# Queries of two batches from seven block products for eight, the second batch's queries and the summed weights kept in DRAM: a fused gated cross-attention and LoRA-MoE kernel

## The chip, the cores and the metric

The kernel runs on one core of one Trainium2 chip. The metric is the device time of one execution in microseconds. The kernel before takes 2636.26 us, the median of three runs (2635.27, 2636.26 and 2637.21).

The engines have short names throughout. PE is TensorE, the matrix engine, and PEld its weight loads. DVE is VectorE, ACT is ScalarE and POOL is GpSimd. SP is SyncE, which issues most of the DMA transfers (SPq is its queue). "Granted clock" is the share of full speed at which TensorE was allowed to run.

## The reference, cut to what matters

Everything is fp32. `x` is (4, 256, 512): four batches of 256 query rows. `ctx` is (4, 1601, 512): 1601 context rows for each batch. There are 32 query heads and 8 key/value heads of 128 columns, so G = 4 query heads share a key/value head.

```python
q = (layernorm(x) @ Wq + bq).reshape(B, L, 8, 4, 128)      # Wq: 512 x 4096
k, v = split(ctx @ Wkv + bkv, 2)                            # Wkv: 512 x 2048
scores = einsum('blkgd,bmkd->bkglm', q, k) / sqrt(128)
o = einsum('bkglm,bmkd->blkgd', softmax(scores), v)
x = x + tanh(g_xattn) * (o.reshape(B, L, 4096) @ Wo + bo)
h = layernorm(x)
w = top-2-of-8 weights of softmax(h @ router_W.T), renormalised
x = x + tanh(g_ffn) * (h @ base_W.T + 2 * sum_e w_e * (h @ A_e) @ B_e)   # rank 16
```

Only the computation of `q` and the handling of the projection weights change here.

## The kernel before, in words

**Tiling.** One group is one batch b, one key/value head h and one tile l of 128 query rows: 4 x 8 x 2 = 64 groups, worked one after another. A group's 4 query heads x 128 rows are the 512 columns of its score products. The 1601 context rows are 12 tiles of 128 and a rest of 65, so a group has 13 score products (`score_unit`) and 13 products of probabilities with values (`av_unit`). The maximum over the context rows is folded tile by tile on DVE and spread over the partitions (`fold`, `spread`). Then DVE subtracts it (`sub`, L925) and ACT takes the exponent (`exp`, L928). An fp32 product takes two passes, which are two MATMUL records in the trace.

**Order of the work.** `run_group` puts the score products of one group on PE, in turns with the AV products of the group before. After it, `window` puts filler on PE, until about RATE ns of it have been placed: keys, values and queries that later groups need, and the output projection of the group before. Filler is a list of `Task`s, each a list of steps with a cost and, for some, a due window. The orders of PE, DVE and ACT are written out by hand (`tc.manual_schedule`). At build time, a planner keeps a model clock for each engine (`clock`) and decides in which order instructions are emitted. Work for DVE and ACT is put off into named queues by `later` ("sub", "oT", "exp", "ln", "T", "sum", "low"). `pump` emits pieces as the model clock passes them; `force` emits what a piece needs, along with pieces of other queues that fit before it within FIT ns. On the chip, each engine works strictly through the order that came out of this.

**Keys and values.** Most of them are made with the Strassen-Winograd scheme: a product of 2x2 blocks takes seven block products and some additions instead of eight block products (`pair_steps`, L645). The blocks of the weight are two heads by two halves of the 512 input features (A11, A12, A21, A22). The other factor is split by the same halves of the features and by two halves of the context rows. Four sums of weight blocks (`weight_sums`, L306: S1, S2, S4 and S3, which overwrites A21) and the sums of context blocks (`ctx_sums`) are made on DVE, in queue "T". The results pass through PSUM banks named `px`, `py` and `pz`. ACT copies a finished one out, and DVE adds a bank to what was copied (`copy_to`, `add_to`). The key and value weights are loaded again and summed again for every batch (`load_pair`, L293).

**Queries.** `q_steps` (L532) makes the queries of one key/value head in one batch: 4 heads x 4 chunks of 128 features, as 16 plain products of 256 columns into the banks `pq`, and ACT copies each with its bias into `qT` (L547). `load_wq` (L282) loads the 1 MB of weights of a head. `x_steps` (L383) loads the x of a batch, layer-normalises it (`layernorm`: statistics on DVE, the root on ACT, then reciprocal and normalisation on DVE, all by `later`), transposes it on PE (`transpose_rows`, L248, bank `pt_x`) and copies it out on DVE as `xnT`.

**The start.** For batch 0, the kernel transposes context tiles as they land (`turn_ctx`), and makes the keys and values of the first head pair by plain products (`pk`, `pv`) as soon as a tile allows it. From the seventh tile on it adds the x steps, and then come the four query products of head 0 and the first scores. The loads of the start are all issued at once, mostly on SP, in the order context tiles, value weights, more context tiles, x, query weights.

## Time and profile before

| | before |
|---|---|
| median of three runs | 2636.26 us |
| profiled execution | 2636.84 us |
| its span | 2635.1 us |
| mean granted TensorE clock | 0.999 |
| PE busy | 2608.0 us, 99%, 9125 instructions |
| PEld busy | 1480.3 us, 56% |
| DVE busy | 2090.8 us, 79%, 2991 instructions |
| ACT busy | 1187.5 us, 45%, 1896 instructions |
| POOL busy | 96.4 us, 4%, 400 instructions |
| DMA | 104.71 MB, mean 40 GB/s |
| score products (L889) | 775.6 us |
| AV products (L979) | 766.1 us |
| query products (L540) | 231.5 us, 1024 records |
| output projection (L1052) | 231.5 us, 512 records |

Busy time is the time in which at least one instruction of the engine was running. Loads of PE weights run beside products and are counted apart. The span goes from the first to the last instruction of the profiled execution, which lasted 1.7 us longer than its span. A row of the group list gives source line, engine, operation, output and inputs with their shapes, the count, busy time, mean duration of one, and the idle time that lay ahead of it with what ended it. Records of products overlap each other, so a mean duration of a product is a latency and not the distance from one product to the next.

### The profile page before, as it was taken

The page shows a single profiled execution, that of the slowest core. Times are in us where ns is not written, and L with a number is a line of the kernel's source. Part 1 is how long each engine was busy: PE and PEld are TensorE (multiplying, and loading weights), DVE is VectorE, ACT ScalarE, POOL GpSimd, SP SyncE. Part 2 cuts the span into 40 slices and gives each one's busy share as a digit, 9 for nine tenths or more (in the row PEclk, how much of TensorE's full clock was granted, in tenths as well). Part 3 has the DMA queues.
Part 4 walks back from the last instruction along what each step waited for, and adds up shares of the span by engine and source line. Part 5 has one row for each costly group of instructions (what it writes and reads, how often), then busy time and mean ns, then how long its engine had stood idle before and what let it go on. Part 6 is the DMA issues. An engine that isn't in the chain of part 4 may idle for free.

```text
span 2635.1 us, 25287 instructions
## 1 busy us (share of the span) xinstructions
PE 2608.0 (99%) x9125; PEld 1480.3 (56%) x9125; DVE 2090.8 (79%) x2991; ACT 1187.5 (45%) x1896; POOL 96.4 (4%) x400
## 2 busy tenths in 40 slices
PE   8999999999999999999999999999999999999998
PEld 6555565655646555565555646555565555646544
DVE  2787877888878887878878878888878878878886
ACT  2544444454444444446444444445544444444441
POOL 0000000000000000000000000000000000000000
PEclk9999999999999999999999999999999999999999
DMA  4101101120111101112001111002111011101100
GB/s 148 35 9 40 40 33 40 41 75 24 40 32 41 37 12 40 40 33 90 24 24 41 40 32 41 26 23 69 61 33 41 8 40 41 39 33 40 49 1 32
DMA packets 78150, 104.71 MB, mean 40 GB/s; under 512 B 3228, under 2 KB 36028, under 8 KB 78024
## 3 DMA queue, kind: packets, MB, share of 16 engines
q1 hardware_dynamic: 76632, 102.01, 12.1%
q8 instruction: 72, 1.18, 0.2%
q0 software_dynamic: 336, 0.55, 0.1%
q10 hardware_dynamic: 1056, 0.52, 0.1%
q14 instruction: 54, 0.44, 0.1%
HBM read 100.98 MB, written 2.10 MB: 39 GB/s over the span
## 4 chain that ended last, share of the span: by engine, by line
PE 80%; DVE 12%; ACT 5%; issue 1%; POOL 1%; DMA 0%; ACTq 0%; POOLq 0%; DVEq 0%
PE av L979 21%; PE sc L889 21%; PE po L1052 8%; PE pq L540 7%; PE pxk L674 5%; PE pxv L685 4%; PE pk L584 3%; DVE p L925 3%; ACT p L896 3%; PE pyk L674 2%; PE pyv L685 2%; DVE sm L821 2%; DVE mx L821 2%; ACT p L928 1%; PE pzk L674 1%
## 5 line engine op out<-in xcount | busy, mean ns | idle before, releaser
L889 PE MATMUL sc<-qT,kT 128*128 128x512 f32 (+1 forms) x1664 | 775.6, 592 | 1.3 <-ACT qT L547 1.3
L896 ACT COPY p<-sc 65x512 f32<-65x512 f32 x820 | 464.5, 589 | 680.4 <-PE sc L889 399.9
L979 PE MATMUL av<-p,v 65*128 65x512 f32 x1640 | 766.1, 592 | 2.0 <-ACT p L928 2.0
L979 PEld LDWEIGHTS av<-p,v 65*128 65x128 f32 x1640 | 309.5, 190 | 382.6 <-issue 378.2
L889 PEld LDWEIGHTS sc<-qT,kT 128*128 128x128 f32 (+1 forms) x1664 | 307.1, 186 | 375.2 <-issue 339.8
L821 DVE TENSOR_TENSOR mx<-mx,p 128x1024 f32<-128x1024 f32 x252 | 308.8, 1225 | 228.2 <-ACT p L896 225.8
L928 ACT ACTIVATE p<-p 65x512 f32<-65x512 f32 x442 | 434.4, 995 | 112.5 <-DVE p L925 104.8
L925 DVE TENSOR_TENSOR p<-p,mb 65x512 f32<-65x512 f32 x442 | 481.3, 1137 | 0.2
L821 DVE TENSOR_TENSOR sm<-sm,p 128x1024 f32<-128x1024 f32 x252 | 307.1, 1218 | 1.2
L1052 PE MATMUL po<-wo,oT 128*128 128x512 f32 x512 | 231.5, 595 | 0.0
L540 PE MATMUL pq<-xnT,wq 128*128 128x256 f32 x1024 | 231.5, 379 | 0.0
L540 PEld LDWEIGHTS pq<-xnT,wq 128*128 128x128 f32 x1024 | 193.2, 190 | 38.8 <-issue 5.1
L1052 PEld LDWEIGHTS po<-wo,oT 128*128 128x128 f32 x512 | 95.3, 191 | 103.1 <-issue 98.9
L712 ACT ACTIVATE kT<-pxk,biasT 128x384 f32<-128x384 f32 (+1 forms) x120 | 60.7, 526 | 183.2 <-PE pxk L674 183.2
L715 ACT COPY v<-pxv 128x384 f32<-128x384 f32 x120 | 56.9, 474 | 172.6 <-PE pxv L685 172.6
L838 POOL COPY quad_sm<-quad_sm 32x16 f32<-32x16 f32 x186 | 48.2, 259 | 2288.6 <-DVE quad_sm L834 2247.0
L815 DVE TENSOR_TENSOR mx<-p,p 128x1024 f32<-128x1024 f32 x63 | 77.2, 1226 | 58.5 <-ACT p L896 58.5
L547 ACT ACTIVATE qT<-pq,biasT 128x256 f32<-128x256 f32 x128 | 60.5, 473 | 136.5 <-PE pq L540 135.6
L685 PEld LDWEIGHTS pxv<-wv,ctxT 128*128 128x128 f32 x720 | 88.7, 192 | 20.2 <-issue 17.2
L685 PE MATMUL pxv<-wv,T 128*128 128x128 f32 x720 | 91.4, 277 | 4.2 <-ACT v L715 4.2
L584 PE MATMUL pk<-ctxT,wk 128*128 128x417 f32 (+1 forms) x256 | 91.7, 513 | 2.8 <-ACT ctxT L250 1.5
L685 PEld LDWEIGHTS pxv<-wv,T 128*128 128x128 f32 x720 | 86.3, 192 | 7.3 <-ACT v L715 6.5
(211 smaller groups left out, 2251.1 us busy)
## 6 DMA issues: line engine op xcount, KB each, us to landing
wq<-in_L_xattn_Wq_dram SPq DMA_DIRECT2D x32, 1024.0 KB, 5.2
wo<-in_L_xattn_Wo_dram SPq DMA_DIRECT2D x32, 1024.0 KB, 5.1
ctx<-in_ctx_dram SPq DMA_DIRECT2D x36, 256.0 KB, 2.6
wk<-in_L_xattn_Wkv_dram SPq DMA_DIRECT2D x30, 256.0 KB, 2.9
wv<-in_L_xattn_Wkv_dram SPq DMA_DIRECT2D x30, 256.0 KB, 3.3
ctx<-in_ctx_dram SPq DMA_DIRECT2D x6, 512.0 KB, 11.7
xa<-in_x_dram SPq DMA_DIRECT2D x4, 512.0 KB, 11.3
out_dram<-xa SPq DMA_DIRECT2D x8, 256.0 KB, 2.0
```

The costliest lines, as they stand in the source:

```text
L540: nc.tensor.matmul(pq[:, :L], w_t["q", b, h][:, c, g * HDIM : (g + 1) * HDIM], xnT_t[b][:, c, :], start=(c == 0), stop=(c == NC - 1),)
L584: nc.tensor.matmul(pk[:, :n], w_t["k", b, h // 2][:, raw_slot(h % 2, c), c % 2, :], ctxT_t[b][:, c, lo : lo + n], start=(c == 0), stop=(c ...
L674: nc.tensor.matmul(bk[:, :n], a(SLOT[i], c), operand(i, c, s, n), start=first and c == 0, stop=c == 1, skip_group_check=True,)
L685: nc.tensor.matmul(bk[:, t * HDIM : (t + 1) * HDIM], operand(i, c, s + t * P, P), a(SLOT[i], c), start=first and t == 0 and c == 0, stop=c ...
L815: nc.vector.tensor_tensor(acc, p[first], p[first + 1], op)
L821: nc.vector.tensor_tensor(acc, acc, p[j], op)
L889: nc.tensor.matmul(sc[:r, :], kT_t[b, h][:, key_col(i) : key_col(i) + r], qT_t[b, h][:, :, l * P : (l + 1) * P], start=True, stop=True,)
L896: nc.scalar.copy(p[:r, k, :], sc[:r, :])
L925: nc.vector.tensor_tensor(p, p, m, ALU.subtract)
L928: nc.scalar.activation(p, p, AF.Exp, scale=scale)
L979: nc.tensor.matmul(av, v_t[b, h][:r, i, :], p_t[key][j][:r, k, :], start=(j == 0 and k == 0), stop=(j == NPAIR - 1 and k == len(pairs[j]) ...
L1052: nc.tensor.matmul(po, oT_t[key][:, g, :], w_t["o", b, h][:, g, :], start=(g == 0), stop=(g == G - 1),)
```

## The change: what it does

- `x_steps` handles two batches at once (JOINT = 2). Their normalised, transposed x lie side by side in one tile `xq`, together with three sums; a fourth overwrites a block. The sums are made on DVE in queue "ln". x of batches 2 and 3 is made from head 3 of batch 1 on.
- The queries are made by `pair_steps("q", ...)`: the blocks of the weight are two heads by two halves of the features, and the columns' halves are the two batches. Fourteen products of 256 columns give two heads of two batches. The first batch's results go to `qT`, the second's to a tile `qs` and from there to DRAM, from where `load_q` reads them when their batch is worked. So `q_steps` comes only in batches 0 and 2, in every window, as a `first` task.
- `keep` writes a weight with its sums to DRAM when it is first used. `load_pair` reads it back in later batches, and `weight_sums` is left out then. The query weights' sums are made in queue "ln".
- RATE is 9700 for 10700, and `force` lets pieces of queue "sub" fit within 1200 ns.
- At the start, query weights of two pairs are loaded and their sums are put in the queue ahead of the context tiles; the x steps come from the fourth tile on; each key and value step comes one tile later; two query pairs precede the first scores.
- Space: the bias row `bo` goes into `qs`; tiles of the last part (`ones`, `fT`, `lm`, `midT`, `lm6`, the last output weight) lie in the tiles of `xq` and `wq`. Six early transposes of the feed-forward part are copied by ACT instead of DVE.

The core of the diff:

```diff
-            for other in queues.values():
+            for name, other in queues.items():
+                fit = 1200 if name == "sub" else FIT
...
-    def load_pair(kind, b, hp, tile_=None, eng=nc.sync):
+    def load_pair(kind, b, hp, tile_=None, eng=nc.sync, tag=None):
...
+        if (kind, hp) in kept:
+            eng.dma_start(w.rearrange("p s c f -> p (s c f)"), kept[kind, hp])
+            done["w", kind, b, hp] = clock["now"] + LAG_PAIR
+            return
+        src, lo = (wq, 0) if kind == "q" else (wkv, KVD if kind == "v" else 0)
...
+    def keep(kind, b, hp):
+        if (kind, hp) in kept or b == B - 1:
+            return
+        kept[kind, hp] = d = dram.tile([P, 14 * HDIM], F32, tag=f"w{kind}_{hp}", name=f"kept_{kind}_{hp}")
+        nc.sync.dma_start(d, w_t[kind, b, hp].rearrange("p s c f -> p (s c f)"))
 
     def weight_sums(kind, b, hp):
+        if ("w", kind, b, hp) in done:
+            return
...
-                "T", "v", 420, clock["now"] + LAG_PAIR,
+                "ln" if kind == "q" else "T", "v", 420, clock["now"] + LAG_PAIR,
...
+    JOINT = 2
+    TQ = JOINT * L // 2
+    XQ = NC * 2 * TQ + 6 * TQ
...
+        def sums():
+            xt, T = xnT_t[b], Tx_t[b]
+            b11, b12, b21, b22 = (xt[:, c : c + 2, k : k + TQ] for c in (0, 2) for k in (0, TQ))
+            for out_, x_, y_ in (
+                (T[:, 0], b12, b11),
+                (T[:, 1], b22, T[:, 0]),
+                (T[:, 2], b21, T[:, 1]),
+                (b12, b22, b12),
+            ):
+                later(
+                    "ln", "v", 160 + 2.1 * TQ, clock["v"],
+                    lambda o=out_, x=x_, y=y_: nc.vector.tensor_tensor(o, x, y, ALU.subtract),
+                    ("T", "q", b) if out_ is b12 else None,
+                )
...
-    def q_steps(b, h):
...
+    def load_q(b, h):
+        new_q(b, h)
+        for g in range(0, G, 2):
+            nc.sync.dma_start(qT_t[b, h][:, g : g + 2, :], q_kept[b, h, g])
...
@@ pair_steps
+            if is_q:
+                g = h0 % G + f
+                if JOINT == 1:
+                    return [(qT_t[b, h0 // G][:, g, half * TQ : half * TQ + n], bk[:, :n])]
+                if half == 0:
+                    return [(qT_t[b, h0 // G][:, g, :], bk[:, :n])]
+                return [(second["q"][:, f, :], bk[:, :n])]
...
-                over()
+                if i == 1 and s == parts0:
+                    keep(kind, b, hp)
+                    if is_q:
+                        if hp % 2 == 0:
+                            new_q(b, hp // 2)
+                        if JOINT == 2:
+                            second["q"] = pool.tile([P, 2, L], F32, tag="qs", name=f"qs_{nm}", bufs=1)
...
+                        nc.sync.dma_start(d, second["q"])
+                over()
...
-            done["xT", nm] = transpose_rows(xn, P, xT, f"f_{nm}")
+            done["xT", nm] = transpose_rows(xn, P, xT, f"f_{nm}", i is not None)
...
-    RATE = 10700
+    RATE = 9700
...
+    def q_steps(b, h, i):
...
+            if (b, hp) == (0, 0):
+                next_weights("q", 0, 2)
+            elif hp + 1 < NHEAD // 2 and (b, hp) != (0, 1):
+                next_weights("q", b, hp + 1)
+
+        return pair_steps("q", b, hp, then)[0]
...
-    load_wq(*heads[0])
+    load_pair("q", 0, 0)
+    load_pair("q", 0, 1, tag="wo")
...
+    ks, vs = plain_k_steps(0, 0), plain_v_steps(0, 0)
+    for i in range(NL):
+        weight_sums("q", 0, i)
...
-        if n >= 6 and xs:
+        if n >= 3 and xs:
             xs.pop(0)[2]()
-        if (n_k + 1) * SUB <= (i + 1) * P and i < FULL:
+
+        if (n_k + 1) * SUB <= i * P and i < FULL:
...
-    for f in qs:
-        spend(f[0])
-        f[2]()
-    load_wq(*heads[1])
+    for i in range(NL):
+        tasks.append(Task(q_steps(0, 0, i)))
+    flush(lambda t: True)
...
-            if h == NKV - 2 and l == 1 and b + 1 < B:
-                tasks.append(Task(x_steps(b + 1), now + 1))
+            if (h, l) == (NKV - 5, 1) and b + 1 < B and (b + 1) % JOINT == 0:
+                load_pair("q", b + 1, 0)
+                tasks.append(Task(x_steps(b + 1), now + 7))
...
-                tasks.append(Task(q_steps(*nxt), hi * NL + NL - 1))
+            if nxt is not None and nxt[0] % JOINT == 0:
+                tasks.append(Task(q_steps(*nxt, l), now, first=True))
+            elif nxt is not None and l == 0:
+                load_q(*nxt)
```

## The prediction

> **What bounds the kernel now.** I read the page's busy shares first, then what PE waits for, then single windows, and last the start.
>
> ```profile
> PE 2608.0 (99%) x9125; PEld 1480.3 (56%) x9125; DVE 2090.8 (79%) x2991; ACT 1187.5 (45%) x1896; POOL 96.4 (4%) x400
> ...
> PE pxv L685 <- ACT v L715: 4.2, 12, 0.6
> PE pt_f L248 <- DVE ffn_x L1155: 2.7, 1, 2.7
> ```
>
> PE is busy 99% of the span, and the longest wait in the list of its waits is 4.2 us in total. So the kernel is bound by how much PE has to do. DVE, at 79%, is next.
>
> The second view is the time line of PE, which gives the true rate of the Q projection; the means of the groups (379 ns) are latencies of overlapping instructions.
>
> ```profile
> 599.66 1.89 PE L540 MATMUL pq<-xnT,wq 128*128 128x256 f32 x8
> 601.39 0.60 PE L248 MATMUL pt_x<-ident,xn 128*128 128x128 f32 x4
> ```
>
> Eight records are four fp32 products of 256 columns (two passes each). From start to next start they take 1.73 us: 0.432 us a product. In the same way 512 columns cost 0.858, 417 cost 0.70, 384 cost 0.66 and 128 cost 0.112.
>
> The third view is the windows: a group's 13 score products with the 13 AV products of the group before (22.3 us), then filler (keys, values, Q, output), until the next group's first score. Four windows in a row:
>
> ```profile
> 798.40:842.00 43.60, 43.29 (x202) 28.27 (x201) 36.43 (x52) 20.61 (x33) 2.81 (x12) 1.00 0.07 25
> 842.00:877.90 35.90, 35.90 (x139) 21.02 (x137) 28.56 (x39) 15.36 (x24) 0.00 (x0) 1.00 0.14 44
> 877.90:919.50 41.60, 41.60 (x114) 21.14 (x113) 33.28 (x48) 20.98 (x33) 1.78 (x6) 1.00 0.08 26
> 919.50:955.10 35.60, 35.60 (x97) 18.10 (x96) 27.64 (x38) 13.82 (x22) 1.14 (x6) 1.00 0.14 44
> ```
>
> The columns after the length are PE, PEld, DVE and ACT busy. PE is busy from end to end. My per-product times, added up over the program order, give 43.1, 35.9, 41.7 and 35.8 for these windows, so sums of products are times here. DVE has 7 to 8 us idle in each.
>
> **What is removed: 64 products.** Before, 32 heads x 4 batches x 4 chunks = 512 products of 256 columns. After, two heads and two batches go together: 7 block products of two chunks, 14 for 16. That is 32 pairs x 14 = 448, and the built program has 448 of them, all 128x256. 64 x 0.432 = 27.65 us less PE work. If nothing else moved: 2636.84 (the profiled execution) - 27.65 = 2609.2.
>
> **What it adds off PE.** DVE: 96 additions of 128x256 (nearest rows: 128x384 takes 546 to 558 ns, 128x32 174 to 181; by line 0.42) = 40 us; weight sums go from 108 to 92 (405 ns each) = -6.5; eight sums of x halves at about 0.69 = 5.5. In all +39 us, in the even batches only, where the windows also gain PE work (14 products, 6.05 us, for 8, 3.46 us). ACT: 128 copies of Q before and after, 473 ns each. DMA: 23 stores and 36 loads of kept weights (0.92 MB), 32 stores and 32 loads of Q (0.26 MB), less 33.5 MB of Wq and 10.5 of Wkv, plus 8.4 of Wq in pair form: about 140 MB for 104.7, so the 12.1% share of the queue becomes about 17%. I cost this at nothing. What hides it is that a weight is loaded when the pair before it ends, about 40 us before its first use, and a 1 MB load lands in 5.2 us. On SP each store stands ahead of later loads and waits for sums on DVE. The tightest case is the key load of the second pair in batch 0: it stands behind the store of the fourth Q weight, whose sums lie behind seven subtractions. It is issued some 18.7 us after the last score, lands 4 us later, and DVE takes it up about 24.5 us after it: 2 us spare. Without that cover the folds behind these sums, and then the scores, would be late by the difference.
>
> Inside a Q pair the second block accumulates on the first one's bank, so PE needs ACT's copy of it first. ACT starts 0.20 us after the last product, runs 0.47, and PE resumes within 0.1: 0.75 us, against one product pair of 0.864 between. It fits if ACT is free, which it is at the start of a window (exponents come after the 4 us in which DVE spreads the maximum). Cost between 0 and 3 x 0.1 x 32 = 10 us; I take 1.
>
> **What it moves: the start.** This is where I see the gain go. Before:
>
> ```profile
> 8.58 1.11 PE L248 MATMUL pt_ctx<-ident,ctx 128*128 128x128 f32 x4
> 10.68 5.90 PE L584 MATMUL pk<-ctxT,wk 128*128 128x417 f32 x8 [0.99 <-DVE ctxT L253]
> 30.43 0.63 PE L248 MATMUL pt_x<-ident,xn 128*128 128x128 f32 x4 [1.53 <-DVE xn L272]
> 63.64 6.65 PE L889 MATMUL sc<-qT,kT 128*65 128x512 f32 x15 [0.56 <-ACT qT L547]
> ...
> 26.88 0.20 ACT L275 ACTIVATE sd_x<-sd_x 128x1 f32<-128x1 f32 x1
> 28.94 0.69 DVE L253 COPY ctxT<-pt_ctx 128x512 f32<-128x512 f32 x1 [6.28 <-PE pt_ctx L248]
> 29.55 0.15 DVE L271 RECIPROCAL rs_x<-sd_x 128x1 f32<-128x1 f32 x1
> ```
>
> The last three rows show DVE taking instructions strictly in order: the reciprocal had its input at 27.1 and ran at 29.55, after a copy that waited for PE. In the changed program DVE's order, after its second context copy (done at 10.4), is: eight sums of the first two Q weights, then the first layer norm, then everything else. And PE's order has the first x transpose, which needs that norm, ahead of the first key product. The Q weights are the last loads issued, behind all context tiles and two x tiles.
>
> ```profile
> 8.54 2.02 SPq L388 DMA_DIRECT2D xa<-in_x_dram  x1
> ...
> xa<-in_x_dram SPq DMA_DIRECT2D x4, 512.0 KB, 11.3
> ...
> 12.00:28.00 16.00, 15.21 (x59) 10.65 (x58) 1.63 (x4) 4.61 (x11) 0.00 (x0) 1.00 1.05 398
> ...
> q10 hardware_dynamic: 1056, 0.52, 2.5%
> ```
>
> The first x lands at 8.54 + 11.3 = 19.8. Then 0.52 MB more of x at 398 GB/s, 1.3 us; then 1.05 MB of Wq in rows of 512 bytes (before: 2 KB). q10 carried the key weights in such rows: 2.5% of 16 engines over 70 us for 0.52 MB is 300 GB/s, so 3.5 us. The Trainium skill (DMA: Bandwidth & Descriptors, Specifications) gives full line rate from 512 bytes up: 0.9 us less. I take the trace: both weights are there at 24.6. Four sums of 405 ns: 26.3. Statistics 1.05, root on ACT 0.4, reciprocal, norm and hand-over 0.9: PE goes on at 28.7, where before it went on at 10.7.
>
> From 28.7 to the first score PE has 50.9 us of work: four x transposes 1.8, keys 10.9, values 22.5, context transposes 3.6, Q 12.1. The first key group runs at half rate (5.7 us for 2.8), with the x transpose before it 3.4 us; before too. Each of the three later x transposes waits for a norm whose root stands on ACT behind the value copies: about 2.1 us each, by the rows above (1.53 for the same chain). Another 1.1 for the last key group, 1.5 inside the last Q pair, whose blocks have nothing between them. First score at 28.7 + 50.9 + 3.4 + 9.0 = 92.0, against 63.64: 28.4 later, of which 6.1 is work that is in the sum already (5.2 of Q, 0.9 of x). Stall added: 22 us. Bounds 14 (weights 3 us earlier, half of the later waits) and 29.
>
> A rule speaks against these gaps: by TensorE: Matmul & The Clock Gate (The HAM clock gate, "What's actually happening") an idle window of about 3.4 us drops PE to half clock, and it takes as long to recover. By the rule the three gaps of 2.1 us cost nothing more. The trace is less lenient:
>
> ```profile
> 2524.82 1.57 PE L248 MATMUL pt_f<-ident,ffn_x 128*128 128x128 f32 x8 [2.74 <-DVE ffn_x L1155]
> 2526.18 4.86 PE L1052 MATMUL po<-wo,oT 128*128 128x512 f32 x8
> ...
> 2526.00:2528.00 2.00, 2.00 (x5) 0.96 (x4) 1.78 (x4) 0.00 (x0) 0.00 (x0) 0.50 0.03 8
> ```
>
> A gap of 2.74 us was followed by a granted clock of 0.50 and 4.86 us for what takes 3.60; one of 2.10 us at 2486 was not. I take 0, and keep 3 x 1.7 = 5 for the range.
>
> **The middle and the end.** In batches 1 and 3 Q comes from DRAM, so four windows have 156.7 - 4 x 3.46 = 142.9 us of PE work, 35.7 each; DVE has 125.9 - 8 x 0.405 = 122.7, 30.7 each. Waits on POOL and on copies leave it a little room: 1 us in all. At the end 6.9 us of Q filler are gone from the windows where PE already stands 9.6 us for DVE (time line of PE, 2459 to 2544), but six copies of 0.69 move from DVE to ACT: between -4 and +6, I take +1.
>
> **Sum.** 2636.84 - 27.65 + 22 + 1 + 1 + 1 = 2634.2; the median before is 0.6 below the profiled execution: 2633.6, say 2634. About 5.3 us (0.2%) is what a measurement of this kernel can tell from no change: 2631.0 to 2641.5.
>
> **The rivals.**
> (A, 40%) The sum above: the start eats four fifths of the gain, 2628 to 2641.
> (B, 33%) The start costs half of what I say, because the weights land earlier than first in, first out (two key pieces issued into an empty queue landed after 3.7 and 5.7 us). For: the queue's engines work side by side. Against: x took 10.9 to 11.7 us in this very place. 11 us back: 2623.
> (C, 18%) DVE becomes the bound in batches 1 and 3. For: 30.7 us busy; maximum folds now wait (225.8 + 58.5) / 64 = 4.4 us per window for score copies, POOL 1.0; if these waits stay, 36.1, and with 0.3 for the projections 36.4 is over 35.7. It decides from there: 0.7 x 28 windows = 20 us, 2654. Against: the waits shrink when DVE is late, and up to seven score banks can wait before PE does.
> (D, 9%) Copies inside the Q pairs come late, behind exponents: 0.3 us per pair and more, 2644.
> That the change leaves the products as they were is excluded by the program's own count.
>
> **Numbers.** Faster: B nearly whole and a sixth of A, 0.38. Same: most of A and a little of D, 0.35. Slower: C and most of D, with A's upper edge, 0.27. Range for 8 in 10: 2620 (B with its lower bounds) to 2653 (most of C).
>
> **What would show it.** In the profile after: PE idle about 18 us before its first x transpose, released by DVE xn, with DVE waiting for a DMA of wq; first score near 92; pxq, pyq and pzq together 193.5 us; PE busy near 2580. I am wrong if the first score comes before 84 or if score products in batches 1 and 3 wait for ACT by more than a few us in total. A faster kernel with the start as I say would mean that the end or the middle held a gain that I don't see.

## The result, and the profile after

The changed kernel takes 2706.95 us (median of four runs, 2704.2 to 2708.07), the kernel before 2636.27 beside it. The ratio is 1.0267 (95% interval 1.0249 to 1.0284): 70.7 us slower, where 2634 was forecast and 2653 was the upper end. The profiled execution took 2708.07 us, with a span of 2706.2.

The page of the kernel after, busy times and main DMA queue:

```profile
PE 2608.9 (96%) x8997; PEld 1459.1 (54%) x8997; DVE 2126.3 (79%) x3073; ACT 1177.9 (44%) x1898; POOL 89.5 (3%) x401
...
q1 hardware_dynamic: 73224, 137.27, 15.3%
```

128 records are gone (64 products of two passes), DVE has 35.5 us more (39 forecast) and the DMA queue's share is 15.3% (17 forecast). But PE is busy 96% of the span, no longer 99%, and its busy time has not fallen. Some 19 us of the missing 28 are products that ran at half clock and count longer: PE was busy for 54.1 us at half clock, before for 16.1 (an estimate from the clock and the records of the two traces). The waits of PE (us in total, times, longest):

```profile
PE pt_x L246 <- DVE xn L270: 28.0, 6, 19.6
PE av L1036 <- ACT p L985: 15.1, 7, 5.2
PE sc L946 <- ACT p L953: 11.2, 8, 1.7
PE sc L946 <- DVE oT L1093: 8.7, 7, 2.5
PE pxq L708 <- ACT qT L753: 7.5, 3, 2.5
PE pxv L719 <- ACT v L756: 7.0, 6, 2.0
```

Only the first line belongs mainly to the start (24.9 of its 28.0 us). Before, no wait came to more than 4.2 us in total; now score and AV products wait too. In batches 1 and 3 score products wait 10.6 us for ACT, before not at all: one of the two signs of being wrong that the prediction had named.

**Where the time went.** I cut both traces into windows, from a group's first score (the product of 65 rows) to the next group's, and compared each window's length with its PE work: the products in program order by the distances that the prediction used (512 columns 0.858 us, 417 0.70, 256 0.432, and so on; 384 with 0.665, 128 in a block product 0.2235). What is left over is called excess below. The method overstates the context transposes at each batch boundary by some 6 us, nearly alike in all kernels; hence the negative entries. Done again with 0.112 us for every transpose, the boundaries come to -0.4 each before and to 0.2, 11.9 and 2.9 after, and no difference in the table moves by more than 1.0 us.

| part | before, excess | after, excess | difference |
|---|---|---|---|
| start, to the first score | 8.4 | 28.3 | +19.9 |
| batch 0 (windows 1 to 13) | 0.8 | 23.3 | +22.5 |
| boundary 0/1 (14, 15) | -7.2 | -5.6 | +1.6 |
| batch 1 (16 to 29) | 1.4 | 25.5 | +24.1 |
| boundary 1/2 (30, 31) | -7.2 | 5.5 | +12.7 |
| batch 2 (32 to 45) | 1.0 | -1.3 | -2.3 |
| boundary 2/3 (46, 47) | -7.2 | -3.0 | +4.2 |
| batch 3 (48 to 61) | 0.8 | 15.2 | +14.4 |
| end (62 to 64) | 13.0 | 15.4 | +2.4 |
| PE work | 2631.8 | 2603.5 | -28.3 |

Together 71.2, against 71.1 between the spans. The removed work is there in full: 128 records, 64 products of 0.432 us, are 27.65 us; where the table's other 0.65 comes from is open. The start took 19.9 back. The other 77 us went in the middle, where the prediction had 2.

**The start** (time line of the kernel after: start, duration, engine, line, what, and in brackets the idle time before it and its releaser):

```profile
9.45 0.69 DVE L251 COPY ctxT<-pt_ctx 128x512 f32<-128x512 f32 x1 [0.46 <-PE pt_ctx L246]
24.50 3.35 DVE L324 TENSOR_TENSOR wq<-wq 128x256 f32<-128x256 f32 x8 [14.35 <-DMA wq<-in_L_xattn_Wq_dram]
...
27.76 0.69 DVE L263 BATCH_NORM_STATS2 st_x<-xa 128x6 f32<-128x512 f32 x1
...
29.92 1.12 PE L246 MATMUL pt_x<-ident,xn 128*128 128x128 f32 x4 [19.65 <-DVE xn L270]
...
40.97 0.63 PE L246 MATMUL pt_x<-ident,xn 128*128 128x128 f32 x4 [1.76 <-DVE xn L270]
...
90.43 11.37 PE L946 MATMUL sc<-qT,kT 128*65 128x512 f32 x26 [0.52 <-DVE qT L762]
```

DVE stands 14.35 us in front of the weight sums, though its next instruction, the statistics of x, needs only x. PE stands 19.65 us behind it.

**The middle** (windows of the kernel after; columns: length, busy time of PE, PEld, DVE, ACT and POOL, granted clock, DMA share, GB/s). Two windows of batch 0, four of batch 1, four of batch 2:

```profile
196.68:229.76 33.08, 33.08 (x93) 17.26 (x92) 25.44 (x37) 12.26 (x22) 1.14 (x6) 1.00 0.16 49
229.76:293.64 63.88, 58.49 (x281) 39.64 (x280) 53.42 (x77) 25.17 (x41) 3.37 (x12) 0.97 0.24 85
...
797.45:833.01 35.56, 35.56 (x89) 16.59 (x88) 29.88 (x44) 15.58 (x27) 1.14 (x6) 1.00 0.11 29
833.01:867.80 34.79, 34.79 (x90) 16.58 (x89) 30.04 (x44) 14.63 (x24) 1.14 (x6) 1.00 0.06 22
867.80:903.36 35.56, 35.39 (x145) 20.79 (x144) 29.42 (x41) 15.80 (x26) 1.14 (x6) 1.00 0.12 42
903.36:944.83 41.47, 39.42 (x163) 22.82 (x161) 35.58 (x46) 19.42 (x31) 1.14 (x6) 0.96 0.12 42
...
1433.13:1474.73 41.60, 41.60 (x117) 21.80 (x116) 33.05 (x48) 19.35 (x31) 0.81 (x5) 1.00 0.12 41
1474.73:1515.56 40.83, 40.83 (x117) 21.80 (x116) 32.77 (x48) 18.78 (x29) 1.48 (x8) 1.00 0.13 47
1515.56:1556.74 41.18, 41.18 (x174) 25.94 (x173) 32.27 (x45) 18.33 (x29) 1.14 (x6) 1.00 0.16 52
1556.74:1599.66 42.92, 42.92 (x191) 27.63 (x189) 31.42 (x44) 18.81 (x31) 1.54 (x6) 1.00 0.20 68
```

In batch 2, with Q as filler, PE is busy from end to end. In batch 1, without Q, three windows look full and the fourth is too long: the four take 147.4 us for 142.5 of PE work. DVE is busy for 124.9 us of the same four windows and idle for 22.5; together that is their length, 36.85 a window. Most of the idle part is waiting inside the softmax. DVE's waits in these four windows of the kernel after, then in the four windows of before that the prediction shows:

```profile
DVE mx L878 <- ACT p L953: 10.5, 9, 1.2
DVE sm L905 <- POOL quadm_sm L902: 3.3, 4, 0.8
DVE mx L872 <- ACT p L953: 1.9, 4, 0.5
...
DVE mx L821 <- ACT p L896: 13.7, 14, 1.5
DVE mx L815 <- ACT p L896: 3.8, 4, 1.2
```

The waits of the maximum folds for score copies fell from 17.5 to 12.4 us in four windows, 4.4 to 3.1 a window. Waits for POOL take 1.2 a window. So a window needs 31.2 us of DVE work and 4.3 of these waits; another 1.3 is idle time of DVE in smaller pieces. PE has 35.6 us of work: DVE has no room left. Over the whole span the fold waits look unchanged, 279.2 us for 284.3 before; by batch they went from 4.6 a window to 3.6 and 3.7 in batches 1 and 3, and to 5.1 in batch 2.

That the full-looking windows already lose ground is seen on DVE's time line, in the normalisation of the previous group's output:

```profile
804.73 0.69 DVE L1093 TENSOR_TENSOR oT<-av,sm 128x512 f32<-128x512 f32 x1
...
842.34 0.69 DVE L1093 TENSOR_TENSOR oT<-av,sm 128x512 f32<-128x512 f32 x1
...
878.18 0.69 DVE L1093 TENSOR_TENSOR oT<-av,sm 128x512 f32<-128x512 f32 x1
...
914.74 0.69 DVE L1093 TENSOR_TENSOR oT<-av,sm 128x512 f32<-128x512 f32 x1
```

Its end comes 8.0, 10.0, 11.1 and 12.1 us after the four windows' starts (before: 8.0, 1.9, 5.8 and 5.0, with no such climb). In the fourth, PE notices (time line of the kernel after):

```profile
907.17 2.47 DVE L878 TENSOR_TENSOR sm<-sm,p 128x1024 f32<-128x1024 f32 x2
908.47 0.58 ACT L953 COPY p<-sc 65x512 f32<-65x512 f32 x1 [1.86 <-DVE sm L878]
909.11 3.34 PE L946 MATMUL sc<-qT,kT 128*128 128x512 f32 x4 [1.75 <-ACT p L953]
...
916.86 2.05 ACT L953 COPY p<-sc 128x512 f32<-128x512 f32 x4 [5.09 <-DVE sm L872]
```

DVE is still summing the previous group's probabilities. Until it has, ACT has no place to copy scores to, the score banks stay full, and PE waits. After it the lag is back at 7.9, and the four-window cycle starts again. In batch 1 the last five windows (25 to 29) lose 20 us, in batch 3 the last five (57 to 61) lose 9: the layer norms and copies of x for batches 2 and 3 put 10.5 us of DVE work into windows 25 to 29. That is where batch 1's extra loss stands; no run isolates it.

In batch 0 it is the unevenness. The window of 33.08 us has little filler, the next gets 55.8 us of PE work. DVE falls behind in the short one, and the copies of Q in the long one come late: its pxq waits 2.49 us for ACT, as the prediction's rival D had it for all Q pairs.

### The profile page after: what moved, and what is told of

It is laid out like the page before. It is cut to its first block, busy times and chain, and to the rows that moved or that the text cites. A ratio compares the mean times of both kernels' runs of the same rounds, so it can differ in the third digit from the quotient of the medians.

```text
span 2706.2 us, 25416 instructions
## 1 busy us (share of the span) xinstructions
PE 2608.9 (96%) x8997; PEld 1459.1 (54%) x8997; DVE 2126.3 (79%) x3073; ACT 1177.9 (44%) x1898; POOL 89.5 (3%) x401
## 3 DMA queue, kind: packets, MB, share of 16 engines
q1 hardware_dynamic: 73224, 137.27, 15.3%
## 4 chain that ended last, share of the span: by engine, by line
PE 74%; DVE 18%; ACT 4%; issue 2%; POOL 1%; DMA 1%; SPq 0%; ACTq 0%; POOLq 0%; DVEq 0%
PE av L1036 20%; PE sc L946 19%; PE po L1109 6%; DVE p L982 5%; PE pxv L719 5%; PE pxq L708 4%; PE pxk L708 4%; DVE sm L878 3%; PE pyv L719 3%; ACT p L953 3%; PE pk L614 2%; DVE mx L878 2%; PE pyq L708 2%; PE pyk L708 2%; ACT p L985 1%
## 5 line engine op out<-in xcount | busy, mean ns | idle before, releaser
L946 PE MATMUL sc<-qT,kT 128*128 128x512 f32 (+1 forms) x1664 | 788.0, 598 | 21.3 <-ACT p L953 11.2
L953 ACT COPY p<-sc 65x512 f32<-65x512 f32 x820 | 458.5, 590 | 784.9 <-PE sc L946 334.4
L1036 PE MATMUL av<-p,v 65*128 65x512 f32 x1640 | 774.5, 598 | 16.2 <-ACT p L985 15.1
L1109 PE MATMUL po<-wo,oT 128*128 128x512 f32 x496 | 223.0, 592 | 1.7 <-ACT oT L1096 1.7
L708 PE MATMUL pxq<-xq,wq 128*128 128x256 f32 x512 | 134.3, 386 | 8.4 <-ACT qT L753 7.5
L708 PEld LDWEIGHTS pxq<-xq,wq 128*128 128x128 f32 x512 | 94.7, 193 | 44.2 <-issue 18.6
L872 DVE TENSOR_TENSOR mx<-p,p 128x1024 f32<-128x1024 f32 x63 | 77.2, 1226 | 40.9 <-ACT p L953 40.8
L719 PE MATMUL pxv<-wv,ctxT 128*128 128x128 f32 x720 | 89.5, 275 | 0.0
```

Source lines behind the costliest of these rows:

```text
L708: nc.tensor.matmul(bk[:, :n], a(SLOT[i], c), operand(i, c, s, n), start=first and c == 0, stop=c == 1, skip_group_check=True,)
L719: nc.tensor.matmul(bk[:, t * HDIM : (t + 1) * HDIM], operand(i, c, s + t * P, P), a(SLOT[i], c), start=first and t == 0 and c == 0, stop=c ...
L872: nc.vector.tensor_tensor(acc, p[first], p[first + 1], op)
L946: nc.tensor.matmul(sc[:r, :], kT_t[b, h][:, key_col(i) : key_col(i) + r], qT_t[b, h][:, :, l * P : (l + 1) * P], start=True, stop=True,)
L953: nc.scalar.copy(p[:r, k, :], sc[:r, :])
L1036: nc.tensor.matmul(av, v_t[b, h][:r, i, :], p_t[key][j][:r, k, :], start=(j == 0 and k == 0), stop=(j == NPAIR - 1 and k == len(pairs[j]) ...
```

## The experiments

Two theories stood at first. (M) The middle is lost because DVE, with its own waits, needs longer per window than PE has left, in batches 1 and 3 by the missing Q work and in batch 0 by uneven windows. (S) The middle is lost to something that the change added: the Q pairs' copies, the stores and loads of kept weights, or too few buffers. Edits are against the changed kernel unless another is named. Where only one run is given, it is one profiled execution; differences of a few microseconds are then read from its windows and not from its total. The change also lowered RATE and let pieces of queue "sub" fit within 1200 ns; no run sets either back by itself.

**The start.** First the weight sums alone, later in DVE's queue:

```diff
-    for i in range(NL):
-        weight_sums("q", 0, i)
...
+        if n == 8:
+            for k in range(NL):
+                weight_sums("q", 0, k)
```

> The changed kernel with one thing moved: the eight sums of the first two Q weights are queued at the ninth context tile instead of ahead of the layer norms; the x steps still begin at the fourth tile. Theory (the start waits for Q weights and then for x): PE resumes near 24 us instead of 29.9, because the first x lands at 19.8, the three later waits of 1.7 us stay, first score near 85 (90.4 in the changed kernel), 2701 us in all. Rival (the sums are not what delays the norms; x itself or the queue is late): first score still within 1 us of 90, 2707.

One run: 2701.12 us, the first score at 85.2 (90.4 without the edit). As expected. Then with the x steps later as well (`n >= 3` becomes `n >= 6`):

> As the run before it, and the x steps begin at the seventh context tile, as in the kernel before the change. Theory: no gap of over 3 us is left at the start; first score at 71 (63.6 before the change, plus 5.0 of Q, 0.9 of x and 1.5 inside the last Q pair), so 19 us less than the changed kernel: 2688. Rival (the start is not a cost of its own: what it loses is lost again later, because DVE is behind there too): the first score comes earlier and the total stays above 2700.

2694.13 us, ratio 1.0219 (1.0202 to 1.0236), first score at 79.0, excess of the start 16.9. That is less than was hoped for, because the sums now stand ahead of the second norm (time line of this run):

```profile
31.93 3.25 DVE L324 TENSOR_TENSOR wq<-wq 128x256 f32<-128x256 f32 x8
35.10 0.68 DVE L263 BATCH_NORM_STATS2 st_x<-xa 128x6 f32<-128x512 f32 x1
...
37.35 1.09 PE L246 MATMUL pt_x<-ident,xn 128*128 128x128 f32 x4 [6.07 <-DVE xn L270]
```

The stall of the start is the order of DVE's queue. Changing it here gives back 12.8 us of 70.7, and the middle stays.

**Batch 0.** Longer windows there, so that the short one is filled:

```diff
-        left = RATE
+        left = 12000 if now < NKV * NL else RATE
```

> The changed kernel with the filler budget of a window set to 12000 in batch 0 alone (9700 elsewhere), so that by the program order the windows of batch 0 hold 44, 46, 38.5, 44 us of PE work instead of 35, 43, 33, 56. Theory (a window shorter on PE than the softmax chain of DVE, about 36 us, leaves DVE late, and the next window's score and Q copies on ACT come late for PE): the 23.7 us by which the fourth windows of batch 0 exceed their PE work (8.1, 8.7, 6.9) fall below 5, total 2686. Rival (the copies inside Q pairs are late by themselves, wherever they stand): the waits of 2.5 us in front of pxq stay, total 2705.

2693.56 us, ratio 1.0216 (1.0201 to 1.0232). The excess of batch 0 fell from 23.3 to 3.0 as forecast, so uneven windows are its cause. The total gained less than the 20, because the boundary windows 14 and 15 lost 7.1. Windows 4 and 5, and 15, of this run:

```profile
196.46:242.07 45.61, 45.61 (x214) 30.37 (x213) 36.91 (x57) 18.38 (x31) 1.69 (x9) 1.00 0.20 70
242.07:280.56 38.49, 38.49 (x150) 23.26 (x149) 28.32 (x39) 17.13 (x28) 0.57 (x3) 1.00 0.14 48
...
654.78:709.42 54.64, 49.99 (x124) 24.30 (x125) 44.53 (x63) 24.00 (x39) 4.39 (x13) 0.94 0.16 58
```

Windows 4 and 5 are now PE from end to end; what was packed early leaves a heap of DVE work for the boundary.

**Batches 1 and 3, less work for DVE.** In these two batches, two of the seven pairs of score tiles are left out of the maximum that is subtracted before the exponent. It is only a shift, and the sums are over all rows; but rows that are left out are no longer guarded against overflow. That takes 2.44 us of DVE work from each window. In the first version the planner still counts them (it is returned 1220 ns), so that the order of the instructions stays:

```diff
         elif j > first + 1:
+            if op == ALU.max and key[0] % 2 == 1 and j in (3, 4):
+                return 1220
             nc.vector.tensor_tensor(acc, acc, p[j], op)
```

> The changed kernel in which two of the maximum folds on DVE (1.22 us each) are left out for every group of batches 1 and 3, so the maximum there is taken over fewer context rows; PE's order is the same to the instruction. DVE has 2.4 us less to do in each of 30 windows. Theory (in batches 1 and 3 DVE with its waits sets the length of a window, 36.9 us on average against 35.6 of PE work, and the end of batch 1 too): of the 53 us by which windows of batches 1 and 3 exceed their PE work 40 go, total 2665. Rival (loads of Q and kept weights from DRAM, or the halved clock after gaps, set it): no more than 10 us go, total 2697 or above.

One run: 2683.0 us. The excess of batches 1 and 3 fell from 40.7 to 17.6, not to nothing: 2.4 us stayed in every fourth window, where DVE's order is still the one written for the longer stream. With the planner told (`return 0`):

> As e3_relief (two maximum folds left out for each group of batches 1 and 3), but now the planner of the order knows that they cost nothing, so the instructions behind them on DVE may be placed earlier. PE's windows in these batches stay as they are. Theory (in e3_relief the order on DVE, written for the longer stream, held the subtractions behind additions that wait for PE, and that kept 2.4 us in every fourth window): the excess of batches 1 and 3 falls from 53 in the changed kernel to below 12, total 2660. Rival (the order has no part in it): as e3_relief, 2683.

One run: 2646.66 us, better than expected. The excess of batches 1 and 3 is 0.3 and -0.4, and that of windows 30 and 31 fell by 9.9 as well. The third and fourth window of the same cycle in this run:

```profile
866.16:901.29 35.13, 35.13 (x146) 20.72 (x145) 29.52 (x41) 16.91 (x26) 1.13 (x6) 1.00 0.14 42
901.29:938.17 36.88, 36.88 (x163) 22.42 (x161) 30.58 (x42) 18.21 (x29) 1.13 (x6) 1.00 0.14 47
```

41.47 us became 36.88, all of it PE. The copies of Q, the stores, the loads and the number of buffers are as they were. DVE is what set these windows.

**The kept weights undone.** Weights are loaded and summed again for every batch:

```diff
     def keep(kind, b, hp):
-        if (kind, hp) in kept or b == B - 1:
-            return
+        return
```

> The changed kernel without kept weights: every batch loads the raw weights and sums them on DVE again; Q of the second batch still goes by DRAM. DMA drops by 31 MB, DVE gains eight sums of 405 ns for every four windows of batches 1 to 3 (0.8 us a window). Theory (DVE is what batches 1 and 3 wait for): 0.8 us more for each of their 30 windows and later value weights besides, 2730. Rival (the stores and loads of weights are what delays the windows): below 2695.

One run: 2734.97 us. The stores and loads cost less than the DVE sums that they save; batches 1 and 2 rose by 20 and 15, while the boundary between them fell by 10.7.

**One batch at a time.** The same seven products for eight, but with the columns' halves inside one batch, so that every window has its Q work. This comes with the later sums and x steps, with longer windows in batch 0, and with the x of a batch made at the end of the one before:

```diff
-    JOINT = 2
+    JOINT = 1
...
-        left = RATE
+        left = 12000 if now < NKV * NL else RATE
...
+            if nxt is not None and nxt[1] == 0:
+                if l == NL - 1:
+                    tasks.extend(Task(q_steps(*nxt, i), now) for i in range(NL))
```

> Q by seven products for eight within each batch (blocks of 128 columns, halves of one batch's rows), so no Q goes to DRAM and every batch has the same filler; weights are still kept in DRAM. x of a batch is made at the end of the batch before, as in the kernel before the change; Q weight sums at the eleventh context tile, x steps from the seventh, budget 12000 in batch 0. PE work by the program order and the measured rates is 2610.8 (2603.5 in the changed kernel, 2631.8 before). Theory (windows of 35.6 us are shorter than DVE's 36.9; here PE has 38 to 40 in each): no stall in batches 1 to 3, first score before 66, 2625 in all, 11 us less than before the change. Rival (the seven-product Q pairs stall PE by their copies wherever they stand): 0.5 us or more in each of 64 windows, 2655.

2702.02 us, ratio 1.0252 (1.0236 to 1.0267): far from the forecast. The steady windows of batches 1 to 3 (38 to 40 us) stalled no more, as (M) says, but windows 16, 32 and 48, just behind the boundaries, lost 20.2, 13.9 and 12.9, and batch 0 lost 43.9. Both Q pairs of a boundary had been put into one window, and the second waits for its weights, which is 5.0 of window 32's 13.9 (time line of this run):

```profile
1370.73 1.22 PE L711 MATMUL pxq<-xq,wq 128*128 128x128 f32 x4 [5.00 <-DMA wq<-kept_q]
```

A variant of this kernel has ten buffers of probabilities where nine were, and RATE unchanged in batch 0 (`NBUF = NPAIR + AHEAD + 2`):

> As e5_single, with ten buffers for score tiles instead of nine (the smaller x tile leaves room) and no special budget in batch 0. Theory (DVE waits for score copies on ACT, which wait for buffers that DVE's own sums release; one more buffer loosens this loop): DVE's idle time in front of maximum folds falls by a third or more against e5_single, total 2620. Rival (the number of buffers is not what paces the loop): idle time in front of maximum folds as in e5_single, total within 5 us of it.

2689.25 us, ratio 1.0202 (1.0185 to 1.0219). DVE's idle time in front of the maximum folds is 235.2 us, for 233.4 without the buffer: more buffers move the wait and do not take it away. Since RATE changed with them, the total of this run says nothing on buffers, and more buffers in the two-batch kernel were not tried. Then, against the first of these two, one Q pair in each of the two boundary windows, and longer windows only in the first five:

```diff
-        left = 12000 if now < NKV * NL else RATE
+        left = 12000 if now < 5 else RATE
...
-            if nxt is not None and nxt[1] == 0:
-                if l == NL - 1:
-                    tasks.extend(Task(q_steps(*nxt, i), now) for i in range(NL))
-            elif nxt is not None and nxt[0] % JOINT == 0:
+            if nxt is not None and nxt[0] % JOINT == 0:
                 tasks.append(Task(q_steps(*nxt, l), now, first=True))
```

> As e5_single, with the pairs of the next batch's first head placed one a window like all others (in e5_single both stood in the batch's last window, the second waiting 5 us for its weights) and the budget of 12000 in the first five windows only. By the program order the windows of batch 0 hold 38 to 40 us of PE work from the seventh on. Theory (a window longer than DVE's stream has no stall, here 38.0 by 36.9 plus four more additions; batch 0 has 2.4 us of weight sums a window on top and still stalls): excess of batches 1 to 3 below 5 in all, of batch 0 12 to 20, total 2635. Rival (batch boundaries stall for another reason, such as context sums): 12 us and more at each, total 2665.

2659.44 us, ratio 1.009 (1.0073 to 1.0107). Batches 1, 2 and 3 have excesses of 0.0, 1.7 and 1.6, with no DVE work taken away. What keeps it above the kernel before is batch 0 (22.8) and the boundaries (windows 15, 31 and 47 with 6 to 7 each). One steady window, and window 31 with the wait in it (windows, then time line of this run):

```profile
740.78:779.47 38.69, 38.69 (x118) 19.71 (x117) 32.25 (x48) 17.29 (x31) 1.13 (x6) 1.00 0.12 38
...
1255.77:1302.44 46.67, 42.31 (x141) 23.76 (x140) 38.35 (x58) 21.05 (x34) 1.67 (x7) 0.96 0.09 27
```

```profile
1288.20 3.88 ACT L988 ACTIVATE p<-p 128x1024 f32<-128x1024 f32 x4
...
1295.52 0.71 PE L711 MATMUL pxq<-xq,wq 128*128 128x128 f32 x4 [3.96 <-ACT qT L756]
```

A copy of Q stood behind four exponents on ACT. That is the prediction's rival D; in this kernel it shows at the boundaries and not in every pair.

**The sums of weights on POOL.** The last kernel, with `nc.gpsimd.tensor_tensor` for `nc.vector.tensor_tensor` in `weight_sums` and a cost of 0 for DVE:

> As e9_balanced, with all weight sums (92 in the program, most of them in batch 0) on POOL instead of DVE; POOL is 97% idle. Theory: batch 0 no longer exceeds its PE work by more than 5 us after its first window, total 2620, 16 us less than before the change. Rival (POOL's sums stand in front of its small copies in the softmax sums, or slow DVE's access to memory): batch 0 stalls as in e9_balanced or more, 2635 to 2650.

2677.74 us, ratio 1.0157 (1.0142 to 1.0172): worse, batch 0 at 39.2. The group list of this run (busy and mean ns of one, idle time before it, releasers):

```profile
L324 POOL TENSOR_TENSOR wq<-wq 128x256 f32<-128x256 f32 x64 | 81.6, 1295 | 363.2 <-DMA wq<-in_L_xattn_Wq_dram 311.3 <-PE sc L949 26.6 <-PE pzv L722 23.9
```

These sums take 1295 ns in the mean, for 405 to 420 on DVE, and POOL stands 311.3 us for weights with the small copies of the softmax queued behind it: DVE's waits for those copies rise from 82.1 to 111.2 us, the longest from 1.1 to 8.2. There is a second cost. In this run 38 DVE instructions took over 0.2 us more than the median of their kind, 19.2 us in all. Every one of them overlaps a weight sum on POOL, and the kernels before and after and the one that this run started from have none. How the loss divides between the two was not tested.

The same on the changed kernel, with the x steps as in the second experiment, the sums at the thirteenth context tile and longer windows in the first five:

> The changed kernel (two batches at once) with the same three repairs: x steps from the seventh tile, weight sums on POOL, budget 12000 in the first five windows. Batches 1 and 3 keep their windows of 35 to 37 us. Theory: the start loses 8 us less or more (first score at 72), batch 0 loses nothing, and batches 1 and 3 with their boundaries still lose about 55: 2603.7 + 1.7 + 10 + 55 + tail 13 - 15 for context transposes = 2668. Rival (weight sums were what made DVE late in batches 1 and 3 too): below 2640.

2668.42 us, ratio 1.0123 (1.0108 to 1.0138). The total is as forecast, its parts are not: the first score came at 66.8 and not 72, and batch 0 still loses 8.2. Batches 1 and 3 (20.8 and 15.1) and the boundary 1/2 (5.5) stay. Then, in this kernel, the residual addition of the output projection in batch 3 goes from DVE to ACT and POOL:

```diff
-            nc.vector.scalar_tensor_tensor(
-                xa_t[b][:, l, :], po, tgx, xa_t[b][:, l, :], ALU.mult, ALU.add
-            )
...
+                nc.scalar.activation(part, po, AF.Identity, scale=tgx)
+                t = act(600)
+                nc.gpsimd.tensor_tensor(xa_t[b][:, l, :], xa_t[b][:, l, :], part, ALU.add)
```

> As e11_joint_pool, and in the first five heads of batch 3 the addition of the attention output to x (0.74 us on DVE in each window, and 0.4 us of waiting for PE in front of it) is done by ACT (scaling from PSUM) and POOL (addition). DVE's need there falls from 36.9 to about 35.8 us a window for 35.6 of PE work. Theory: the 4.6 us of excess in windows 53 and 57 fall below 1.5. Rival (DVE's length is not it; the second window of value products stalls by itself): they stay above 3.5.

One run: 2675.11 us, the excess of batch 3 up from 15.1 to 21.4: the forecast failed. But DVE was not relieved (time line of this run):

```profile
2311.47 3.80 POOL L1120 TENSOR_TENSOR xa<-xa,part 128x512 f32<-128x512 f32 x1 [28.93 <-ACT part L1118]
...
2314.18 1.64 DVE L911 TENSOR_TENSOR sm<-sm 128x512 f32<-128x512 f32 x1
```

That DVE instruction takes 0.69 us in the mean of the kernel without this edit. Nine of POOL's ten additions overlap one DVE instruction that is about 1 us longer than usual, more than the 0.74 us saved, so that DVE's busy time in windows 52 to 60 went from 287.5 to 289.7 us. DVE's waits for POOL did not grow (56.0 and 56.2 us). So this run does not test DVE's share by taking work away; that batch 3 lost more with DVE's load no lighter doesn't speak against (M).

**Both mends together.** The shorter maximum of batches 1 and 3, planner told, on the kernel with sums on POOL:

> e11_joint_pool (two batches at once, start, weight sums and the budget of the first windows repaired) with the maximum of batches 1 and 3 taken over five of the seven score tiles, as in e8_relief2, the planner told. Theory (what the change loses is the start, the short windows of batch 0, and DVE's length in batches 1 and 3; with all three repaired the saving on PE comes through): excess over PE work no more than 10 to 15 in all, of which the start 5, total 2615, about 21 us less than before the change. Rival (a further loss lies behind these and appears when they go, such as Q's copies or the loads from DRAM): 2635 or more.

2612.05 us (2610.76 to 2612.8), ratio 0.9911 (0.9896 to 0.9925): faster than the kernel before by 22.6 us. From its page:

```profile
PE 2578.5 (99%) x8997; PEld 1451.2 (56%) x8997; DVE 2038.8 (78%) x2917; ACT 1187.2 (45%) x1894; POOL 207.5 (8%) x493
```

PE is busy 99% again, and only now is its busy time near the 2580 that the prediction gave for the kernel after. But part of this comes from the lighter maximum itself, so the kernel before was given the same. First with the planner told:

> The kernel before the change with the same shorter maximum in batches 1 and 3, the planner told. PE has the same work as before, 2631.8. Theory (there PE sets the windows, and only the end, where PE waits for DVE, gains): 5 to 10 us less in the last three windows, nothing elsewhere, 2628. Rival (DVE costs the kernel before the change as well, so the shorter maximum by itself explains what e8 and e13 gain): 2610 or less.

2678.83 us, ratio 1.0165 (1.0149 to 1.0182), where 2628 was expected. This is no control: the planner, with less DVE time on its model clock, put two output projections into one window, and the second has no weights yet. The waits of PE in this run:

```profile
PE po L1054 <- DMA wo<-in_L_xattn_Wo_dram: 36.4, 7, 5.3
```

Then with the planner not told (`return 1220`), so that PE's order is that of the kernel before:

> The kernel before the change with the shorter maximum in batches 1 and 3 (five of seven score tiles), the planner not told, so that PE's order is exactly the one of before. In e14 the planner, once told, put two output projections into one window seven times, and the second waited 5.2 us for its weights each time, so e14 is no control. Theory (before the change PE sets all windows but the last three): batches 0 to 3 as before within 1 us each, the last three windows 5 to 9 us shorter, 2628. Rival (DVE's length costs the kernel before the change too): batches 1 and 3 together 10 us or more shorter, 2615.

2626.81 us, ratio 0.9968 (0.9956 to 0.9981), as expected: 8.7 us from the lighter DVE alone, 5.7 of them at the end. So some 14 us of the mended kernel's gain are left for the change with its repairs, about half of the 28 removed (22.6 less 8.7, each against the kernel before run beside it; 14.8 by 2626.81 - 2612.05). The control is not perfect: it has neither the repairs of the start and of the first windows nor a planner that was told. The rest lies in batch 0 (8.2 before the relief, 7.2 with it) and the boundaries.

## Why the prediction was wrong

**The step that failed** is in "The middle and the end": "Waits on POOL and on copies leave it a little room: 1 us in all." It measured 77 (with the copies in the Q pairs, another 1 us of the sum). Three parts of it:

- Batches 1 and 3, 38.5 us. Rival C had the mechanism: DVE with its waits against PE's work, 36.4 against 35.7 us a window. The windows took 36.85 for 35.6 of PE work. The sum is nearly right and its parts are not: DVE's busy time was 31.2 (30.7 forecast), the fold waits 3.1 (4.4), those for POOL 1.2 (1.0), the rest 1.3 (0.3). I gave it 18% because "the waits shrink when DVE is late". They did shrink, from 4.6 to 3.6 and 3.7 us a window in batches 1 and 3, and it was not enough. Nor did the score banks save it: they delay a stall by some windows, but a DVE that loses 1 to 2 us in each arrives at it in the fourth. Its price of 20 us came out at 38.5. The difference of 1.25 us a window (36.85 - 35.6) times 28 is 35, against the 0.7 a window that rival C had. Batch 3 lost 10 less than batch 1, because the x steps of batches 2 and 3 stand in batch 1 alone, as far as the windows show.
- Batch 0, 22.5 us. I looked at no window of it. A window of 33.1 is followed by one of 55.8 us of work. The experiment with longer windows in batch 0 took this away.
- The boundaries, 18.5 us, mostly windows 30 and 31, where the sums of the new context (7.8 us of DVE in window 31) and of x for batch 2 (4.9 in window 30) fall on a DVE that is late already: with DVE relieved they fell by 9.9 of 12.7.

**The other steps.**

| step of the sum | forecast | measured |
|---|---|---|
| removed products | -27.65 | -28.3 (all PE work) |
| start | +22 | +19.9 |
| copies in the Q pairs, and the middle | +1 and +1 | +77.2 |
| end | +1 | +2.4 |
| kept weights | 0 | no cost seen (undone, slower) |

The start was right in kind and size: weight sums from 24.5 (24.6 forecast), PE on at 29.9 (28.7), first score at 90.43 (92.0). In part that is luck. The first x landed at 21.55 (19.8 forecast), and of the weights, both due at 24.6, the last piece came at 26.14, just before the fifth sum began at 26.16. All eight sums preceded the norm where my arithmetic had four, which is 1.7 us more, and the later waits were shorter (1.76 for 2.1). The 300 GB/s for 512-byte rows, from the trace of before, was the better guide than the full line rate of the Trainium skill (DMA: Bandwidth & Descriptors, Specifications), by which, by an estimate, the weights were due at 23.7: while such rows made up most of the transfers, from 20 to 23 us, the queues moved 233 to 297 GB/s, for 389 to 401 from 12 to 18. Rival B, that the weights land sooner, is out. The copies in the Q pairs cost nothing where windows are long and even: batch 2 has an excess of -1.3. In batch 0 they were 7.5 us of PE's waits.

**The clock.** I took 0 for stretches at half clock. They did occur: after the start they took 20.4 us of full-speed PE time in batches 0 to 3 (twelve stretches of 3.4 us at 0.50), where the kernel before had none. That bounds their part in the 77 us from above, but it is not all a loss: the same window of the cycle in batch 3 had a granted clock of 1.00 and is as long as the one in batch 1 with 0.96 (kernel after):

```profile
903.36:944.83 41.47, 39.42 (x163) 22.82 (x161) 35.58 (x46) 19.42 (x31) 1.14 (x6) 0.96 0.12 42
2199.01:2240.47 41.46, 37.99 (x162) 22.16 (x161) 35.57 (x46) 19.33 (x30) 1.14 (x6) 1.00 0.13 42
```

Where DVE sets the window, a slow PE just fills what would have been idle. The low clock follows the stalls; it does not make them.

## What to carry to other kernels

Before work is taken from the bounding engine, add up the next engine's busy time and its handshake waits for the windows that lose the work, and compare that with what is left there. Don't count on the waits to vanish once that engine is late: here they shrank by 1 us of 4.6. And read them by stage, since their sum over the span hid even that. Look at every stage: a saving that falls on half of the windows makes the other half's neighbours uneven, and a lag of 1 to 2 us a window is invisible until the buffers between are used up. And where a queue runs strictly in order, what is put ahead of a wait for a late load must be nothing that others need.

## What the runs showed of the hardware that was not expected

- In the kernel after, all changes of the granted clock lie on one grid of 3.413 us. From 70 us on, each step of the grid at full speed in which PE stood idle for 1.75 us or more was followed by half clock (14 steps), and none with 1.69 us or less was. It is the idle time inside one step that counted, not the length of the gap: one of 2.03 us lay inside a step at 446 us and the clock fell; ones of 2.03 and 2.02 us at 272 and 621 lay across two steps and it didn't. In all traces of this case together the limit is less sharp: the least idle time before a fall was 1.39 us, the most without one 2.01. By the Trainium skill (TensorE: Matmul & The Clock Gate, The HAM clock gate) an idle window of about 3.4 us drops the clock, so its length of recovery is met here and its length of idleness is not.
- While POOL worked on an addition, some DVE instructions took longer: 0.69 us became 1.64, and 1.22 became 2.30. In the four kernels with additions on POOL 38 to 50 DVE instructions took over 0.2 us more than the median of their kind, 19 to 29 us in all, and every one of them overlaps such an addition. The kernels before and after have no additions on POOL and no such instruction.
- On POOL, an addition of 128x256 took 843 to 1383 ns in the means of its groups, on DVE 405 to 420; one of 128x512 took 1338 to 7147 ns on POOL (median 1566), where DVE takes 740 for multiplication and addition together. The profile's times on POOL are rough.
